# Last state product shared by three batches and added on VectorE, own products made ahead of the state

## The chip, the cores and the metric

The kernel runs on one core of one Trainium2 chip. All matrix products are in float32. The metric is the device time of one execution in microseconds (us); of several runs the median is taken. The engines are named as in the profile: PE is TensorE's matmul, PEld its weight load, DVE is VectorE, ACT is ScalarE, POOL is GpSimd, SP is SyncE, which issues the DMAs.

## The reference

Two layers act on x of 8 batches, 512 positions and 128 features. Each has an attention part and a feed-forward part with a layer norm, a modulation by a condition and a gated residual. Layer 0 has an RWKV mixing and a linear map with quantised operands, layer 1 a three-branch attention with 16 heads. The change touches only the last part, layer 1's feed-forward, a recurrence over the batches (B, with T = 512 rows each):

```python
def step(c, xt):
    ft = sigmoid(xt @ wf.T + c @ uf.T + bf)
    it = sigmoid(xt @ wi.T + c @ ui.T + bi)
    gt = tanh(xt @ wc.T + c @ uc.T + bc)
    return ft * c + it * gt, None
c_final, _ = lax.scan(step, c0, x)                 # x: the eight batches, one after the other
h = tanh(einsum('tbi,oi->tbo', x, wo) + c_final @ uo.T + bo)
...
h = layernorm(x) * (1 + cb) + sb                   # what the recurrence gets
x = x + gb * _L1_ffn_ref(h, ...)                   # the residual, and the output
```

Every batch's output needs the final state. So for each batch two products meet in a sum: its own, h times wo, and the product of the state with uo, which is the same for all batches.

## The kernel before

Features lie on the 128 partitions and the 512 positions of a batch on the free axis, so a batch is one 128x512 tile and a product of it fills one bank of PSUM. A float32 product of this size stands in the trace as two matmul records.

The main part is a loop over 192 units (batch, head group, kind of attention, rows of queries) in an order written out by hand. Three generators are advanced in its gaps: `layer0` (mixing and linear map of layer 0), `before` (norm and projections of layer 1, `prepare`, which stores a small latent tile through SP, L478) and `recurrence` (`recur`, L553). `recur` normalises a batch after its attention, makes h2 from it (L576), stores it to DRAM in `h2_all` (L578, all batches but the last), forms the three gate products (`of_state` L567 and L584), the gates (L586) and the state `cs2` (L591 to L595). `project` adds the attention's residual, and all batches but the last store their x in `x1_all` (L869).

The code around the change follows this loop (L1027 to L1056). Here a scheduler orders each engine's instructions. SP works through its DMAs strictly in order; a DMA that waits holds those behind it.

- `begin(b)` loads h2 of a batch (L1034) and its x (L1039), and makes the own product into a bank left open for a second product (L1042). The h2 tiles use the buffers qN and k0N of the attention's inputs. The five banks are `o` and `s0` to `s3`; the last batch takes h2 from `recur`.
- After the state, the loop of L1047 runs over the batches: state product into the same bank (L1051), tanh on ACT (L1053) into a tile `oT` (tag qR, two buffers), the gate gb on POOL (L1054), four transposes into one of three banks (L131) and the residual add on DVE (L133) in `add_residual`, and the store of the output (L1056).

PE's order before is: own product of batch 0, transposes of batch 7's attention residual, own product of batch 1, transposes of batch 7's norm (L126), the three gate products (L584), own products of 2, 3 and 4, and then state products, own products of 5, 6 and 7, and transposes mixed.

For the last batch the gate products take banks s0 to s2 and are read there by the tanhs of L586.

Of the kernel before, what the change touches and what calls it, by code (L numbers as in the profile page):

```python
# [11 lines left out]
FP = mybir.dt.float32  # L12
U32 = mybir.dt.uint32
AF = mybir.ActivationFunctionType
ALU = mybir.AluOpType
# [3 lines left out]
B, T, D = 8, 512, 128  # L19
NC = T // 128  # L20
# [3 lines left out]
HG = 4  # L24
# [25 lines left out]
def _views(t, cols):  # L50
    out, at = {}, 0
    for name, n in cols:
        out[name] = t[:, at : at + n]
        at += n
    return out
# [3 lines left out]
def adaln_kernel(ctx: ExitStack, tc: tile.TileContext, x, pa, pb, pc, pt, out):  # L59
    nc = tc.nc  # L60
    V, S, G, PE = nc.vector, nc.scalar, nc.gpsimd, nc.tensor
# [5 lines left out]
    WB, WC, WT = _views(wb, B_COLS), _views(wc, C_COLS), _views(wt, T_COLS)  # L67
# [9 lines left out]
    h2_all = [dram.tile([128, T], FP, name=f"h2all{b}") for b in range(B)]  # L77
    x1_all = [dram.tile([128, NC, D], FP, name=f"x1all{b}") for b in range(B)]
    small = ctx.enter_context(tc.tile_pool(name="small", bufs=2))
    pool_x = ctx.enter_context(tc.tile_pool(name="xs", bufs=5))  # L80
    xs = {}
# [46 lines left out]
    def add_residual(oT, ps, b):  # L128

        for c in range(NC):  # L130
            PE.transpose(ps[:, c * 128 : (c + 1) * 128], oT[:, c * 128 : (c + 1) * 128], ident)  # L131
        xb = xs[b].rearrange("p c d -> p (c d)")
        V.tensor_tensor(xb, ps, xb, ALU.add)  # L133
# [45 lines left out]
    pq = enter(tc.tile_pool(name="l1q", bufs=2))  # L179
    pi = enter(tc.tile_pool(name="l1i", bufs=1))  # L180
    pu = enter(tc.tile_pool(name="l1u", bufs=4))
    ps_s = enter(tc.tile_pool(name="ps_s", bufs=1, space=PSUM))
    ps_t = enter(tc.tile_pool(name="ps_t", bufs=3, space=PSUM))
    ps_o = enter(tc.tile_pool(name="ps_o", bufs=1, space=PSUM))

    def work(i, shape, name):


        return pw.tile(shape, FP, name=name, tag=i)

    def bank(shape, name):
        return ps_t.tile(shape, FP, name=name, tag="t")
# [355 lines left out]
    cs2 = state.tile([128, T], FP, name="cs2")  # L548
# [323 lines left out]
    made_of, latent_of, k1_of, chosen_of, q_of, k3_of, v_of, sel_of, out_of, acc_of, pT_of, rot_of, xnf_of, h2_of = ({} for _ in range(14))  # L872
# [54 lines left out]
    def need(name, b):  # L927
        while (name, b) not in ready:
            advance(M)
# [38 lines left out]
    for i in range(-2, len(units) + 3):  # L968
        un = units[i] if 0 <= i < len(units) else None
        ahead = units[i + 2] if i + 2 < len(units) else None  # L970
# [14 lines left out]
        if un:  # L985
            b, g = un.b, un.g
# [37 lines left out]
    ordered.close()  # L1024


    halves = {}  # L1027
    first = pi.tile([128, HG, T], FP, name="x1_first", tag="p3")

    def begin(b):  # L1030

        if b + 1 < B:
            h2_of[b] = pq.tile([128, T], FP, name=f"h2o_{b}", tag=("qN", "k0N")[b % 2])
            nc.sync.dma_start(out=h2_of[b], in_=h2_all[b])  # L1034
            if b < HG:
                xs[b] = first[:, b, :].rearrange("p (c d) -> p c d", d=D)
            else:
                xs[b] = pool_x.tile([128, NC, D], FP, name=f"x1_{b}", tag="x")
            nc.sync.dma_start(out=xs[b], in_=x1_all[b])  # L1039
        pool, tag = ((ps_o, "o"), (ps_s, "s3"), (ps_s, "s0"), (ps_s, "s1"), (ps_s, "s2"))[b % 5]  # L1040
        halves[b] = pool.tile([128, T], FP, name=f"ho_{b}", tag=tag)
        PE.matmul(halves[b], lhsT=WC["woT"], rhs=h2_of[b], start=True, stop=False)  # L1042

    for b in range(2):
        begin(b)
    need("recur", B - 1)
    for b in range(B):  # L1047
        for ahead in (b + 2, b + 3) if b == 0 else (b + 3,):
            if ahead < B:
                begin(ahead)  # L1050
        PE.matmul(halves[b], lhsT=WC["uoT"], rhs=cs2, start=False, stop=True)  # L1051
        oT = pq.tile([128, 2, T], FP, name=f"oT2_{b}", tag="qR")[:, 0, :]
        S.activation(oT, halves[b], AF.Tanh, bias=WC["bo"])  # L1053
        G.tensor_scalar(oT, oT, mod1[:, 5, b : b + 1], 1.0, ALU.mult, ALU.mult)  # L1054
        add_residual(oT, bank([128, T], f"rp2_{b}"), b)
        nc.sync.dma_start(out=out[b].rearrange("(c p) d -> p c d", p=128), in_=xs[b])  # L1056


def _packs(i):
# [70 lines left out]
```

## Time and profile before

| what | value |
|---|---|
| runs | median 1708.04 us of 3 (1707.66 to 1712.55) |
| profiled execution | 1708.48 us, its span 1706.7 us |
| PE, PEld, DVE, ACT, POOL busy | 92%, 55%, 74%, 68%, 55% of the span |
| granted TensorE clock, mean | 0.96 |
| last gate products begin | 1679.16 us |
| state ready (end of L595) | 1686.14 us |
| first state product | 1686.38 us |
| last residual add | 1702.79 to 1703.48 us |

Times inside an execution count from the start of the span. In lines of the timeline the first number is the start, the second the length, then engine, line, operation and tiles; in brackets is the engine's idle time before it, and what ended that. Lines of the chain have start, length, engine, tile, line and count: the chain is followed back from the last instruction, at each step to what released it. Stretches ("windows") list how long an engine was busy in them and the clock that the throttle granted to TensorE, 1.00 being full speed.

### The profile page before, as it was taken

The numbers are of one execution on the slowest core, as the hardware profiler recorded it, in microseconds if no ns is written. First come the engines' busy times: TensorE is split into PE (matmuls) and PEld (weight loads), VectorE is DVE, ScalarE is ACT, GpSimd is POOL, SyncE is SP. The second block draws the span as 40 slices with busy tenths as digits, with TensorE's granted clock in tenths as the row PEclk, the third lists the DMA queues.
The fourth block names the chain that finished last, engine by engine and source line by source line (L and its number), as shares of the span: only waits on it lengthen the run. The fifth ranks groups of instructions, "written<-read, shape, count | busy, mean of one in ns | idle before, by whom it ended". The sixth has DMA issues, their size and how long they took to land.

```text
span 1706.7 us, 39939 instructions
## 1 busy us (share of the span) xinstructions
PE 1572.7 (92%) x14777; PEld 938.1 (55%) x14777; DVE 1266.0 (74%) x4259; ACT 1152.8 (68%) x3245; POOL 936.8 (55%) x1370
## 2 busy tenths in 40 slices
PE   3388999899999999999899999989999999999997
PEld 2144655465555655655555555655555565665663
DVE  6678878875888868975979768867889667666543
ACT  2244787666776777777666677767776777777882
POOL 2155567554666547554656457654666456655551
PEclk8687999998999999999999999999999999999998
DMA  4000000000000000000000000000000000000012
GB/s 170 1 2 2 2 2 3 7 2 14 3 2 8 7 8 3 1 8 14 3 1 2 7 8 3 2 7 14 3 2 1 14 8 3 1 14 8 14 39 68
DMA packets 13778, 20.55 MB, mean 12 GB/s; under 512 B 912, under 2 KB 9104, under 8 KB 13456
## 3 DMA queue, kind: packets, MB, share of 16 engines
q1 hardware_dynamic: 13584, 17.99, 3.1%
q8 instruction: 118, 1.93, 0.5%
q14 instruction: 76, 0.62, 0.1%
HBM read 11.70 MB, written 5.77 MB: 10 GB/s over the span
## 4 chain that ended last, share of the span: by engine, by line
PE 63%; DVE 26%; ACT 5%; issue 3%; POOL 3%; DMA 0%; POOLq 0%; DVEq 0%; ACTq 0%
PE s L793 19%; PE t L837 12%; DVE p L805 7%; PE o L851 7%; PE s L755 2%; PE k3Rm L638 2%; PE qRm L638 2%; ACT p L814 2%; PE k3Np L610 1%; PE v1p L651 1%; PE op L862 1%; PE o L738 1%; PE qNp L610 1%; ACT pT L603 1%; POOL p L823 1%
## 5 line engine op out<-in xcount | busy, mean ns | idle before, releaser
L823 POOL TENSOR_SCALAR p<-p,rs 128x512 f32<-128x512 f32 (+3 forms) x1024 | 578.8, 586 | 390.9 <-DVE rs L819 221.9
L805 DVE CUSTOM_DVE_ANT_0 p<-s,mask 128x512 f32<-128x512 f32 (+3 forms) x1024 | 442.6, 477 | 178.4 <-PE s L793 178.0
L814 ACT ACTIVATE p<-p,nm 128x512 f32<-128x512 f32 (+3 forms) x1024 | 560.0, 553 | 11.9 <-DVE nm L805 11.8
L603 ACT COPY pT<-t 128x384 f32<-128x384 f32 (+1 forms) x768 | 354.8, 521 | 188.0 <-PE t L837 185.4
L837 PE MATMUL t<-ident,p 128*128 128x128 f32 x2560 | 367.4, 281 | 34.8 <-ACT pT L603 7.2
L837 PEld LDWEIGHTS t<-ident,p 128*128 128x128 f32 x2560 | 276.2, 142 | 160.3 <-issue 115.0
L814 ACT ACTIVATION_READ_ACCUMULATOR p<-p,nm 128x1 f32 x1024 | 197.2, 193 | 0.0
L793 PE MATMUL s<-k3R,qR 32*128 32x128 f32 (+3 forms) x2048 | 188.1, 458 | 4.4 <-DVE nm L805 3.2
L793 PE MATMUL s<-k1R,qR 32*128 32x512 f32 (+3 forms) x2048 | 185.9, 452 | 2.6 <-POOL k1R L625 2.5
L851 PE MATMUL o<-pT,v 128*32 128x512 f32 (+3 forms) x2048 | 153.2, 440 | 0.0
L793 PEld LDWEIGHTS s<-k3R,qR 32*128 32x128 f32 x2048 | 98.8, 188 | 84.4 <-DVE nm L805 30.9
L793 PEld LDWEIGHTS s<-k1R,qR 32*128 32x128 f32 x2048 | 105.4, 186 | 48.5 <-issue 13.6
L851 PEld LDWEIGHTS o<-pT,v 128*32 128x32 f32 x2048 | 60.4, 110 | 111.1 <-issue 100.3
L793 PE MATMUL s<-k0N,qN 32*128 32x512 f32 (+3 forms) x1024 | 102.3, 434 | 0.0
L793 PE MATMUL s<-k3N,qN 32*128 32x512 f32 (+3 forms) x1024 | 96.8, 434 | 0.0
L625 POOL TENSOR_TENSOR k3R<-k3R,rt_k3R 128x512 f32<-128x512 f32 x32 | 40.7, 1272 | 83.9 <-DVE rt_k3R L624 83.9
L805 DVE DVE_READ_ACCUMULATOR2_ANT nm<- 128x1 f32 x1024 | 82.8, 81 | 0.1
L765 POOL TENSOR_TENSOR p<-p,m 128x512 f32<-128x512 f32 x32 | 33.6, 1049 | 67.4 <-DVE m L764 67.4
L638 PE MATMUL qRm<-nqT,wb 96*128 96x512 f32 x128 | 68.8, 621 | 1.2 <-ACT nqT L475 0.7
L793 PEld LDWEIGHTS s<-k0N,qN 32*128 32x128 f32 x1024 | 60.5, 188 | 17.0 <-issue 2.5
L793 PEld LDWEIGHTS s<-k3N,qN 32*128 32x128 f32 x1024 | 55.1, 189 | 22.1 <-issue 15.2
L603 ACT COPY accT<-o 128x512 f32<-128x512 f32 x32 | 18.8, 587 | 71.0 <-PE o L851 71.0
(308 smaller groups left out, 2446.3 us busy)
## 6 DMA issues: line engine op xcount, KB each, us to landing
wb<-pb_dram SPq DMA_DIRECT2D x1, 3731.0 KB, 14.3
x<-x_dram SPq DMA_DIRECT2D x8, 256.0 KB, 3.7
x1all<-x SPq DMA_DIRECT2D x7, 256.0 KB, 2.0
h2all<-h SPq DMA_DIRECT2D x7, 256.0 KB, 2.0
h2o<-h2all SPq DMA_DIRECT2D x7, 256.0 KB, 2.6
x_first<-x1all SPq DMA_DIRECT2D x4, 256.0 KB, 3.6
out_dram<-x_first SPq DMA_DIRECT2D x4, 256.0 KB, 2.2
out_dram<-x SPq DMA_DIRECT2D x4, 256.0 KB, 2.3
```

What stands on the lines that cost most here:

```text
L603: S.copy(dst, src)
L610: PE.matmul(ps, lhsT=w[:, g * 128 : (g + 1) * 128], rhs=src, start=True, stop=True)
L625: G.tensor_tensor(lo, lo, r[0], ALU.subtract)
L638: PE.matmul(ps, lhsT=w[:, i * 128 : (i + 1) * 128], rhs=src, start=True, stop=True)
L755: PE.matmul(sp[h][to, :], lhsT=k[js, g, :], rhs=q[js, h * half : (h + 1) * half], start=(i == 0), stop=(i == 2), skip_group_check=True,)
L765: G.tensor_tensor(p2, p2, m2.unsqueeze(2).to_broadcast([128, T // 32, KEEP]), ALU.subtract)
L793: PE.matmul(un.s[j][:, at : at + n], lhsT=q[js, n - 128 : n], rhs=k[js, 0:n], start=(i == 0 and at == 0), stop=(i == 2), skip_group_check= ...
L805: V.tensor_tensor_reduce(out=un.p[:, j, at : at + n], in0=un.s[j][:, at : at + n], in1=mask[:, T - n :], scale=-1.0, scalar=3.4e38, op0=AL ...
L814: S.activation(p, p, AF.Exp, bias=un.nm[:, j, i : i + 1], scale=-1.0, accum_out=un.rs[:, j, i : i + 1])
L823: G.tensor_scalar(p, p, un.rs[:, j, i : i + 1], 1.0, ALU.mult, ALU.mult)
L837: PE.transpose(tp[:, k, :], un.p[:, j, at : at + 128], ident)
L851: PE.matmul(out_ps[js, c * 128 :], lhsT=v[:, c, js], rhs=pT[:, j, at[0] : at[-1] + 1 : step, :], start=not a and c == 0, stop=False, skip_ ...
```

## The change

- All seven h2 tiles get buffers of their own, those that layer 0's work used (tags l0 to l6), and all loads stand ahead of the products in the program.
- Batches 0, 2, 4, 6 and 7 keep their bank and the two products in it. Batches 1, 3 and 5 have their own product made into one of the three transposes' banks and copied by ACT to SBUF.
- The product of the state with uo is made once more into a bank `uo`; DVE adds it to the SBUF tiles of batches 1, 3 and 5, and tanh reads those.
- Own products of 0, 2, 1, 3 and 5 stand before the last norm on PE, those of 4, 6 and 7 between the gate products and the state.
- The transposes and the residual of a batch follow the tanh of the next in the program.

On PE the order becomes: own product of 0, transposes of the attention residual, own products of 2, 1, 3 and 5, transposes of the norm, gate products, own products of 4, 6 and 7; state product of 0, `uo`, state product of 2, transposes of 0, state product of 4, transposes of 1 and 2, state product of 6, transposes of 3, state product of 7, transposes of 4 to 7. On DVE the three adds of `uo` stand ahead of all eight residual adds. On SP the first five h2 loads stand behind the seventh batch's latent store, the sixth behind the sixth batch's h2 store and ahead of the eighth batch's latent store, the seventh behind the seventh batch's h2 store. Before, they stood behind that one, among the loads of x.

```diff
-    halves = {}
     first = pi.tile([128, HG, T], FP, name="x1_first", tag="p3")
+    for b in range(B - 1):
+        h2_of[b] = work(f"l{b}", [128, T], f"h2o_{b}")
+        nc.sync.dma_start(out=h2_of[b], in_=h2_all[b])
+    for b in range(B - 1):
+        if b < HG:
+            xs[b] = first[:, b, :].rearrange("p (c d) -> p c d", d=D)
+        else:
+            xs[b] = pool_x.tile([128, NC, D], FP, name=f"x1_{b}", tag="x")
+        nc.sync.dma_start(out=xs[b], in_=x1_all[b])
+
+    banks = {0: (ps_o, "o"), 2: (ps_s, "s3"), 4: (ps_s, "s0"), 6: (ps_s, "s1"), B - 1: (ps_s, "s2")}
+    sums = {}
 
     def begin(b):
-        if b + 1 < B:
-            h2_of[b] = pq.tile([128, T], FP, name=f"h2o_{b}", tag=("qN", "k0N")[b % 2])
-            nc.sync.dma_start(out=h2_of[b], in_=h2_all[b])
...
-        pool, tag = ((ps_o, "o"), (ps_s, "s3"), (ps_s, "s0"), (ps_s, "s1"), (ps_s, "s2"))[b % 5]
-        halves[b] = pool.tile([128, T], FP, name=f"ho_{b}", tag=tag)
-        PE.matmul(halves[b], lhsT=WC["woT"], rhs=h2_of[b], start=True, stop=False)
-
-    for b in range(2):
-        begin(b)
+        if b in banks:
+            pool, tag = banks[b]
+            sums[b] = pool.tile([128, T], FP, name=f"ho_{b}", tag=tag)
+            PE.matmul(sums[b], lhsT=WC["woT"], rhs=h2_of[b], start=True, stop=False)
+        else:
+            ps = bank([128, T], f"ho_{b}")
+            PE.matmul(ps, lhsT=WC["woT"], rhs=h2_of[b], start=True, stop=True)
+            sums[b] = work(f"p{b // 2}", [128, T], f"hs_{b}")
+            S.copy(sums[b], ps)
+
+    for b in (0, 2, 1, 3, 5):
+        begin(b)
     need("recur", B - 1)
-    for b in range(B):
-        for ahead in (b + 2, b + 3) if b == 0 else (b + 3,):
-            if ahead < B:
-                begin(ahead)
-        PE.matmul(halves[b], lhsT=WC["uoT"], rhs=cs2, start=False, stop=True)
-        oT = pq.tile([128, 2, T], FP, name=f"oT2_{b}", tag="qR")[:, 0, :]
-        S.activation(oT, halves[b], AF.Tanh, bias=WC["bo"])
+    for b in (4, 6, 7):
+        begin(b)
+    uo = bank([128, T], "uo")
+    oTs = {}
+
+    def finish(b):
+        if b in banks:
+            PE.matmul(sums[b], lhsT=WC["uoT"], rhs=cs2, start=False, stop=True)
+        else:
+            V.tensor_tensor(sums[b], uo, sums[b], ALU.add)
+        oT = oTs[b] = pq.tile([128, 2, T], FP, name=f"oT2_{b}", tag="qR")[:, 0, :]
+        S.activation(oT, sums[b], AF.Tanh, bias=WC["bo"])
         G.tensor_scalar(oT, oT, mod1[:, 5, b : b + 1], 1.0, ALU.mult, ALU.mult)
-        add_residual(oT, bank([128, T], f"rp2_{b}"), b)
-        nc.sync.dma_start(out=out[b].rearrange("(c p) d -> p c d", p=128), in_=xs[b])
+
+    for b in range(B + 1):
+        if b < B:
+            finish(b)
+        if b == 0:
+            PE.matmul(uo, lhsT=WC["uoT"], rhs=cs2, start=True, stop=True)
+        if b:
+            add_residual(oTs[b - 1], bank([128, T], f"rp2_{b - 1}"), b - 1)
+            nc.sync.dma_start(out=out[b - 1].rearrange("(c p) d -> p c d", p=128), in_=xs[b - 1])
```

More of the change, by code (lines that the diff above doesn't have):

```diff
@@ L1024, in adaln_kernel @@
     ordered.close()
-    halves = {}
     first = pi.tile([128, HG, T], FP, name="x1_first", tag="p3")
-    def begin(b):
-        if b + 1 < B:
-            h2_of[b] = pq.tile([128, T], FP, name=f"h2o_{b}", tag=("qN", "k0N")[b % 2])
-            nc.sync.dma_start(out=h2_of[b], in_=h2_all[b])
[L1035 to L1039, printed above, removed]
-        pool, tag = ((ps_o, "o"), (ps_s, "s3"), (ps_s, "s0"), (ps_s, "s1"), (ps_s, "s2"))[b % 5]
-        halves[b] = pool.tile([128, T], FP, name=f"ho_{b}", tag=tag)
-        PE.matmul(halves[b], lhsT=WC["woT"], rhs=h2_of[b], start=True, stop=False)
```

## The prediction

> **What bounds the kernel now.** I read the page first: PE is busy in 92% of the span, so PE work counts nearly everywhere. The diff, however, touches only what follows the last attention, so I then read the chain of work that ended last in the final 40 us, the timeline there, and the granted clock in stretches. The chain, whose columns are start, length and work:
>
> ```profile
> 1671.35 0.59 PE rp L131 x4
> 1671.96 0.70 DVE x L133
> ...
> 1676.65 0.36 DVE xnf L118
> 1677.01 0.04 issue
> 1677.05 1.26 PE tp L126 x4
> ...
> 1679.16 2.07 PE wfT L584 x2
> 1681.23 1.71 PE wiT L584 x2
> 1682.94 1.03 PE wcT L584 x2
> 1683.97 2.58 PE ho L1042 x6
> 1686.54 1.73 PE ho L1051 x4
> ...
> 1702.79 0.69 DVE x L133
> ```
>
> First comes a serial stretch (residual, norm, transposes, three gate products, state). Then, from 1686.4 on, PE has eight state products (L1051), three own products (L1042) and eight groups of transposes (L131). The timeline shows a batch's way through tanh, POOL and the transposes, and that ACT also waits for a transpose group:
>
> ```profile
> 1687.44 0.69 ACT L1053 ACTIVATE oT<-ho,wc 128x512 f32<-128x512 f32 x1 [2.75 <-PE ho L1051]
> 1688.22 0.69 POOL L1054 TENSOR_SCALAR oT<-oT,mod 128x512 f32<-128x512 f32 x1 [25.95 <-ACT oT L1053]
> ...
> 1698.58 0.69 ACT L1053 ACTIVATE oT<-ho,wc 128x512 f32<-128x512 f32 x1 [0.74 <-PE rp L131]
> ...
> 1699.36 0.69 POOL L1054 TENSOR_SCALAR oT<-oT,mod 128x512 f32<-128x512 f32 x1 [0.73 <-ACT oT L1053]
> ```
>
> oT has two buffers, so the tanh of batch b waits for the transposes of b-2. Last the clock, in stretches of 3.41 us (columns: window, length, PE busy, granted clock, DMA share, GB/s):
>
> ```profile
> 82.31:85.72 3.41, 1.54 (x6) 1.00 0.02 5
> 85.72:89.13 3.41, 3.41 (x5) 0.50 0.08 19
> 966.36:969.77 3.41, 1.70 (x26) 1.00 0.00 0
> 969.77:973.18 3.41, 3.05 (x8) 0.50 0.02 5
> 816.17:819.58 3.41, 1.89 (x20) 1.00 0.00 0
> 819.59:823.00 3.41, 2.75 (x56) 1.00 0.00 0
> 1672.92:1676.33 3.41, 0.00 (x0) 1.00 0.41 126
> 1676.34:1679.74 3.40, 1.82 (x5) 0.50 0.00 0
> 1679.74:1683.15 3.41, 3.41 (x5) 0.50 0.00 0
> 1683.16:1686.56 3.40, 3.40 (x9) 1.00 0.17 42
> ```
>
> The clock changes only at the ends of such stretches. A share of PE up to 0.50 (1.70 of 3.41) was followed by half clock, 0.55 (1.89) was not. Back to full it went after a full stretch. The gate products of the last batch run at half clock, because PE pauses from 1672.79 to 1677.05.
>
> **The change part by part.** Unit prices, all from this execution: a 128x512 product holds PE 0.865 (records at 1691.18 and 1692.04); product start to its tanh 1.06 (1686.38 to 1687.44); tanh 0.69, 0.09 to POOL, POOL 0.69, 0.06 to the transposes; these hold PE 0.49 (1698.68 to 1699.17), release DVE's add 0.70 after their start (1702.09 to 1702.79) and the oT buffer 0.76 after it (1697.82 to 1698.58).
>
> *Loads of h2 (seven, L1034 before).* They leave the buffers qN and k0N for those of layer 0's work, so SP issues five right after the seventh batch's latent store (1229.30). They wait for layer 0's last readers of those buffers; the transposes of oTf in the eighth batch end at 1342.53. At 0.32 each they are out by about 1344.2, and the next entry, the sixth batch's x1 store, goes at 1347.24 today. The sixth load stands behind the h2 store of 1370.70, waits about 2.0 for its landing, and has the latent store of 1409.24 behind it; the seventh follows the store of 1540.94. Cost 0: covers of 3 and 36 us. The loads that ran at 1671 and 1685 are gone, and nobody waited for them. The x1 loads keep their places between the same stores.
>
> *Own products of batches 2, 1, 3, 5 ahead of the norm.* PE had batch 1's here, ending at 1672.79; four from 1671.94 end at 1675.40, 1.65 before the transposes of 1677.05. Cost 0; without that cover each would cost 0.865. The three copies to SBUF on ACT (accT's copy of the same shape: 0.587) fall into ACT's idle 7.11 before h at 1678.33: cost 0, or 1.8 uncovered.
>
> *Own products of 4, 6, 7 between gates and state.* Three stand there today too. The last needs the bank of wcT, read by 1684.70; it would start at 1685.7. Cost 0, gain 0.
>
> *After the state.* Take the first state product (1686.38) as 0. Gone are three state products and three own products, added is one (uo): PE has 6 products instead of 11, 4.3 less. But the other engines have a chain of their own. Tanh 0 starts at 1.06, transposes 0 at 2.60 (behind uo and the product of batch 2). uo's sum is out at 1.93; the add for batch 1, 0.69 as the residual add of the same shape, lets tanh 1 start at 2.67, transposes 1 at 4.20. From here every batch waits for the buffer of the one two earlier: 0.76 + 0.69 + 0.09 + 0.69 + 0.06 = 2.29 from transposes to transposes. Batch 2: 4.89; 3: 6.49; 4: 7.18, but the product of batch 7 stands ahead on PE until 7.85; 5: 8.78; 6: 10.14; 7: 11.07. The last add starts at 11.77 and ends at 12.46. The adds for 3 and 5 end at 3.3 and 4.0, before their tanhs (4.96, 7.25); they delay the first residual add by about 0.7, for which nothing waits. Before the last tanh stands 0.34 without a visible cause (its product ended at 1700.20, it began at 1700.58); I keep it: 12.80. Today the same stretch takes 1703.48 - 1686.38 = 17.10. **Gain 4.30**; bounds 4.64 (no such gap) and 3.6 (below).
>
> *The stores of the output.* The last one's issue, landing and program end take 3.2 after the last add today. Stores now come every 1.1 us instead of 1.4 to 2.0; landings go from 2.2 to 3.0 today, so 0 to 0.7 more. I take 0, since the last add follows the one before by 1 us and a store of 256 KB at the 296 GB/s seen at 1701 needs 0.9.
>
> *The clock.* The stretch 1672.92 to 1676.33 now holds 2.48 of PE work and keeps full clock. Then the four transposes take 0.70 instead of 1.28 and the first gate product starts at 1678.58. The stretch to 1679.74 now holds about 0.66 + 1.16 = 1.82 of work, 0.53: between 0.50, which lost the clock, and 0.55, which kept it. If it is lost at 1679.74, the gates end at 1682.62, full clock is back at 1683.15, and three own products end at 1685.48: 0.9 earlier than today. If it is kept, the state is ready at 1683.6 and its first product starts at 1683.8: 2.6 earlier. The phase of these stretches against the program may differ between runs; shifting it through 3.41 us, the same arithmetic gives anything from 0.5 later to 2.6 earlier, with 0.9 near the middle. I take **0.9**, ends -0.5 and 2.6.
>
> **Sum.** 4.3 + 0.9 = 5.2. The profiled execution took 1708.48 (span 1706.7 and 1.8 around it), so it would become 1703.3. It lies 0.44 above the median of the runs, so for a median 1708.04 - 5.2 = **1702.8**. 0.3% of this time, 5.1 us or a border at 1702.9, is about what a measurement of this kernel can tell from no change: the three runs of before reach from 1707.66 to 1712.55.
>
> **Rivals.** *A, above:* shorter tail, clock lost for part of the gates: 1702.8, own range 1702.0 to 1703.5.
>
> *B, the clock stays up.* For it: the pauses left are 1.65 and 0.88. Against it: the share of 0.53, and most phases give a lower one. 4.3 + 2.6 = 6.9, 1701.1. The Trainium skill (TensorE: Matmul & The Clock Gate, Part 1) has the clock fall after an idle window of some 3.4 us; by that, neither pause would cost it and B would be the outcome. The trace agrees on the width, but 82.31 to 85.72 was 45% busy and the clock fell all the same.
>
> *C, no gain from the clock.* The stretch boundary falls so that it is lost at 1677 or 1678. Only the tail gains: 4.3 less 0.3, 1704.0; with slower landings 1704.7.
>
> *D, SP's queue holds the last latent.* This is the slower one. Six loads are queued ahead of the eighth batch's latent store (1409.24), and that batch's first use is its k0N product at 1489.44. Should a load wait for something later than the transposes of 1342.53, PE waits one for one beyond about 1487; the change comes out slower once the queue is held past 1492, and at 1500 it is 1708.04 - 5.2 + 13 = 1715.8. Against it: every reader of those buffers belongs to layer 0, which the eighth batch leaves before its latent exists.
>
> *E, the change does less than it says:* PE stays the bound in the tail, because products and transposes collide. 6 products and 8 groups are 5.2 + 3.9 = 9.1 of 12.5, so this would need 3 us of collisions; 1705 to 1706.
>
> **Chances.** A 0.38, B 0.28, C 0.24, E 0.05, D 0.05. The range takes A, B and C with their bounds: 1700.8 (4.64 + 2.6) to 1705.2 (C at its worst, with some spread of runs). Faster by over 0.3%: B, and somewhat over half of A, and a little of C: 0.54. Within 0.3%: the rest of A and C, and E: 0.40. Slower: D and a disturbed main part, 0.06.
>
> **What would show it.** In the profile after: five h2 loads near 1342 to 1344; PE work until 1675.4 and copies on ACT before h; granted clock 1.00 between 1676.3 and 1679.7 where it was 0.50; a first transposes group about 2.6 and a last add about 12.5 after the first state product; ACT waiting for rp L131, not for ho. Wrong would be: tanhs waiting for DVE, stores landing late, a stretch of half clock inside the tail, or any change before 1671.

## The result, and the profile after

| | before | changed |
|---|---|---|
| runs | median 1710.03 us (1707.34 to 1712.84, 6 runs) | median 1702.41 us (1700.13 to 1705.39, 6 runs) |
| ratio to before | | 0.9958, 95% interval 0.9947 to 0.9970 |
| profiled execution | 1708.48, span 1706.7 | 1705.39, span 1703.6 |

By the ratio the change saves 7.2 us (5.1 to 9.1). By a 2% bound the two are the same; by the 0.3% that this kernel's measurement can tell, the changed one is faster.

The two profiled executions differ by 3.1 only. The profiled one of the changed kernel is the slowest of its six runs, the one of before lies near the fast end of its own. So I cut both traces at events that exist in each: the first transpose of the last attention residual (rp L131), the first state product, and the end of the last residual add.

| us | before | changed | predicted |
|---|---|---|---|
| start to the first residual transpose | 1671.27 | 1673.21 | no change |
| first residual transpose to first state product | 15.11 | 14.69 | 14.21 |
| first state product to end of last add (the tail) | 17.10 | 12.47 | 12.80 |
| last add to the end of the span | 3.19 | 3.22 | 3.19 |
| the three parts behind the first transpose | 35.40 | 30.38 | 30.20 |

The region that the change touches became 5.02 shorter. The rest, 1.94 longer, lies ahead of it; it is taken up below. The chain of the changed kernel that ended last, in the same stretch as the one shown of before (start, length, engine, tile, line, count):

```profile
1673.29 0.59 PE rp L131 x4
1673.91 0.70 DVE x L133
...
1678.59 0.36 DVE xnf L118
1679.08 1.02 PE tp L126 x4
1680.12 0.79 ACT h L576
1680.95 1.25 PE wfT L584 x2
1682.21 1.71 PE wiT L584 x2
1683.91 1.58 PE wcT L584 x2
1685.49 2.58 PE ho L1045 x6
1688.07 0.86 PE ho L1062 x2
1688.93 0.87 PE uo L1073 x2
1689.82 0.70 DVE hs L1064
1690.55 0.73 ACT oT L1066
...
1699.68 0.69 DVE x L133
```

wiT at 1.71 and most of wcT (1.58) still run at half clock; the three own products (ho, 2.58) take 0.86 each. After the state, the chain leaves PE at once, by the sum of batch 1 on DVE (L1064) and its tanh. The timeline of ACT shows what the later tanhs wait for (in brackets the idle time before and its end):

```profile
1690.55 0.72 ACT L1066 ACTIVATE oT<-hs,wc 128x512 f32<-128x512 f32 x1 [0.90 <-DVE hs L1064]
...
1692.85 0.72 ACT L1066 ACTIVATE oT<-hs,wc 128x512 f32<-128x512 f32 x1 [0.92 <-PE rp L131]
1693.53 0.69 ACT L1066 ACTIVATE oT<-ho,wc 128x512 f32<-128x512 f32 x1
1695.15 0.72 ACT L1066 ACTIVATE oT<-hs,wc 128x512 f32<-128x512 f32 x1 [0.94 <-PE rp L131]
1696.46 0.69 ACT L1066 ACTIVATE oT<-ho,wc 128x512 f32<-128x512 f32 x1 [0.58 <-PE rp L131]
1697.46 0.69 ACT L1066 ACTIVATE oT<-ho,wc 128x512 f32<-128x512 f32 x1 [0.32 <-PE rp L131]
```

The four later waits are all for transposes, that is for one of the two oT buffers; only the first is for a DVE add. The stretches of the clock (window, length, PE busy, granted clock, DMA share, GB/s):

```profile
1674.99:1678.40 3.41, 2.32 (x6) 1.00 0.01 2
1678.41:1681.82 3.41, 1.87 (x6) 1.00 0.00 0
1681.83:1685.23 3.40, 3.40 (x5) 0.50 0.00 0
1685.24:1688.64 3.40, 3.40 (x9) 1.00 0.00 0
```

One stretch of half clock is left of two. It follows a stretch in which PE was busy for 1.87 of 3.41, a share of 0.55.

The loads of h2, in the timeline of SP's queue:

```profile
1303.96 40.93 SPq L1030 DMA_DIRECT2D h2o<-h2all  x5
1349.21 0.32 SPq L869 DMA_DIRECT2D x1all<-x  x1
...
1374.71 0.32 SPq L1030 DMA_DIRECT2D h2o<-h2all  x1
```

The last of the five is out at 1344.9. The x1 store follows 1.97 later than before (1347.24 then) and the eighth batch's latent store, at 1411.20, 1.96 later (1409.24 then), which is the 1.94 that this execution is late anyway.

**Where the 1.94 comes from.** accT is the attention's sum, which ACT copies out of PSUM 32 times in the main part. From the start to the first of these copies, in code that the change does not touch, the changed kernel took 179.23 and before 176.78, 2.45 more; from there to the last one 1491.44 and 1491.95. The stretches of the start-up show the clock, first before, then the changed kernel (columns as above, windows of 42):

```profile
42.00:84.00 42.00, 16.01 (x48) 0.60 0.00 0
84.00:126.00 42.00, 36.87 (x237) 0.89 0.01 3
126.00:168.00 42.00, 34.60 (x295) 0.79 0.01 1
```

```profile
42.00:84.00 42.00, 17.95 (x44) 0.54 0.00 0
84.00:126.00 42.00, 36.38 (x193) 0.80 0.01 3
126.00:168.00 42.00, 33.29 (x313) 0.88 0.01 1
```

Between 42 and 126 the clock was lower in the execution of the changed kernel; in the first 168 us it spent 81.9 at half clock, before 75.1. Over the eleven profiles of this study, all with the same start-up, the first accT copy comes between 176.1 and 182.4, and the time at half clock in the first 168 us lies between 71.7 and 95.6; the latest copy (182.4) goes with the most half clock (95.6), but among the others the order is loose (176.1 goes with 75.1 and 78.5, 176.9 with 71.7). So the clock is the likely cause of the late start, and no run tested it. Either way single executions are several us apart before the changed code is reached, and the sum of a change of 5 us has to be read from its own region, or from many runs.

### The profile page after: what moved, and what is told of

Its sections match the earlier page's. It is cut to its first block, busy times and chain, and to the rows that moved or that the text cites. A ratio compares the mean times of both kernels' runs of the same rounds, so it can differ in the third digit from the quotient of the medians.

```text
span 1703.6 us, 39936 instructions
## 1 busy us (share of the span) xinstructions
PE 1571.0 (92%) x14773; PEld 936.0 (55%) x14773; DVE 1267.4 (74%) x4262; ACT 1154.0 (68%) x3248; POOL 936.7 (55%) x1370
## 4 chain that ended last, share of the span: by engine, by line
PE 63%; DVE 26%; ACT 5%; issue 3%; POOL 3%; DMA 0%; POOLq 0%; SPq 0%; ACTq 0%; DVEq 0%
PE s L793 19%; PE t L837 12%; DVE p L805 7%; PE o L851 7%; PE s L755 2%; PE k3Rm L638 2%; PE qRm L638 2%; ACT p L814 2%; PE k3Np L610 1%; PE v1p L651 1%; PE op L862 1%; PE o L738 1%; PE qNp L610 1%; PE k0Np L610 1%; ACT pT L603 1%
```

## The experiments

The theory: the gain is the shorter tail, 4.6, whose new bound is the chain through the two oT buffers, plus part of the gates at full clock. Rivals are that PE's count of products sets the tail, that the loads or the stores take part, and that the pauses are too short to lose the clock. The kernels e1, e2 and e6 were timed once only, so for them the profile counts alone. All columns below are from the profiles of the runs, cut as in the table above.

| kernel | first transpose to state | tail | to the end | sum | half clock ahead of the state |
|---|---|---|---|---|---|
| before | 15.11 | 17.10 | 3.19 | 35.40 | 6.8 |
| changed | 14.69 | 12.47 | 3.22 | 30.38 | 3.4 |
| e8, changed again | 14.69 | 12.48 | 3.23 | 30.40 | 3.4 |
| e1, three products | 14.70 | 16.11 | 3.21 | 34.02 | 3.4, and again in the tail |
| e2, six buffers | 15.98 | 11.57 | 3.20 | 30.75 | 6.8 |
| e3, pause filled | 13.00 | 12.49 | 3.22 | 28.71 | none |
| e4, before, pause filled | 13.00 | 17.11 | 3.20 | 33.31 | none |
| e5, before, early loads | 15.11 | 17.10 | 3.19 | 35.40 | 6.8 |
| e6, six buffers, products ahead | 14.69 | 10.35 | 4.59 | 29.63 | 3.4 |
| e7, e6 and pause filled | 13.00 | 10.35 | 4.50 | 27.85 | none |
| e9, e7, first store earlier | 13.00 | 10.41 | 4.37 | 27.78 | none |

### Without the shared product

Batches 1, 3 and 5 each get a state product of their own in place of `uo`; everything else of the change stays.

```diff
-    uo = bank([128, T], "uo")
...
-            V.tensor_tensor(sums[b], uo, sums[b], ALU.add)
+            own = bank([128, T], f"uo_{b}")
+            PE.matmul(own, lhsT=WC["uoT"], rhs=cs2, start=True, stop=True)
+            V.tensor_tensor(sums[b], own, sums[b], ALU.add)
...
-        if b == 0:
-            PE.matmul(uo, lhsT=WC["uoT"], rhs=cs2, start=True, stop=True)
```

> Each of the batches 1, 3 and 5 gets a state product of its own, in a bank of the transposes, and its add on DVE; the rest stays as changed. PE has 8 state products after the state, not 6. The stretch counts from the start of the first state product to the end of the last residual add: 17.10 us before, 12.47 after. Theory (sharing pays because tanh, POOL, transposes and the two oT buffers form a chain, and every product put into it delays the chain by more than its own time): 15.5. Rival (only PE's own time counts): 12.47 + 2 x 0.865 = 14.2. Rival (sharing is worth nothing, the gain came from the own products moved away): 12.5.

Measured: tail 16.11, one time of 1705.81. Two more products are 1.73 of PE, but the tail grew by 3.64: the products for batches 3 and 5 stand behind transposes on PE, and the tanhs wait for their adds. ACT's timeline:

```profile
1691.27 0.72 ACT L1067 ACTIVATE oT<-hs,wc 128x512 f32<-128x512 f32 x1 [2.52 <-DVE hs L1065]
1691.89 0.67 ACT L1067 ACTIVATE oT<-ho,wc 128x512 f32<-128x512 f32 x1
1695.16 0.72 ACT L1067 ACTIVATE oT<-hs,wc 128x512 f32<-128x512 f32 x1 [2.60 <-DVE hs L1065]
```

Part of the excess is the clock: the stretch from 1695.66 to 1699.07 was busy for 1.38 of 3.41, and the last transposes ran at 0.50.

```profile
1699.00 1.09 PE L131 MATMUL rp<-ident,oT 128*128 128x128 f32 x4 [0.96 <-POOL oT L1068]
```

1.09 instead of 0.66, so 0.43 of the 16.11. Without it 15.7 stands near the 15.5 expected of the chain, and far from both rivals. Hence in this order of PE the sharing carries about 3.2 of the tail's gain of 4.63, and the rest of the change (the own products moved ahead of the state, the new order of the transposes) about 1.4; these two were not taken apart.

### Six oT buffers

```diff
-        oT = oTs[b] = pq.tile([128, 2, T], FP, name=f"oT2_{b}", tag="qR")[:, 0, :]
+        oT = pq.tile([128, 2, T] if b % 3 == 0 else [128, T], FP, name=f"oT2_{b}", tag=("qR", "qN", "k0N")[b % 3])
+        oT = oTs[b] = oT[:, 0, :] if b % 3 == 0 else oT
```

> oT gets six buffers instead of two, the order on PE as the scheduler gives it; the rest stays as changed. Theory (the two buffers set the pace after the change): the same stretch falls from 12.47 to 11.7, no tanh waits for a transposes group any more, and the last batch then waits for its state product, which stands late on PE. Rival (PE or DVE sets the pace already): 12.4 to 12.5.

Measured: tail 11.57, one time of 1704.20. No tanh waits for transposes any more; the last two wait for their state product, since PE's order puts it behind the transposes of earlier batches. ACT's timeline:

```profile
1692.68 0.72 ACT L1067 ACTIVATE oT<-hs,wc 128x512 f32<-128x512 f32 x1
1694.14 0.69 ACT L1067 ACTIVATE oT<-ho,wc 128x512 f32<-128x512 f32 x1 [0.75 <-PE ho L1062]
1696.31 0.69 ACT L1067 ACTIVATE oT<-ho,wc 128x512 f32<-128x512 f32 x1 [1.48 <-PE ho L1062]
```

So the two buffers were the bound of the changed tail, and the price of their chain is 0.90. The gates fared worse in this execution: the clock was lost for two stretches, and the state came 0.87 later than before's. The stretches, columns as in those of the changed kernel:

```profile
1675.21:1678.62 3.41, 1.56 (x6) 1.00 0.00 0
1678.62:1682.03 3.41, 2.62 (x3) 0.50 0.00 0
```

The edit does not touch the gates. What differs is where the stretches lie: here one ends 0.12 after the first residual transpose, in every other profile of the study 1.5 to 2.1 after it.

### The pause filled, with the change and without

Two products that nobody reads (512 and 384 columns) fill PE between the own products and the norm's transposes; in the kernel before, five of them. They are extra work; the outputs do not depend on them.

```diff
     for b in (0, 2, 1, 3, 5):
         begin(b)
+    idle = bank([128, T], "idle")
+    for n in (512, 384):
+        PE.matmul(idle[:, 0:n], lhsT=WC["woT"], rhs=h2_of[0][:, 0:n], start=True, stop=True)
     need("recur", B - 1)
```

> The changed kernel, with two products that nobody reads (512 and 384 columns, 1.5 us) between the own product of batch 5 and the transposes of the last norm, so that PE's pause of 1.65 us ahead of them closes. Theory (the clock is lost in a stretch of 3.41 us in which PE is busy for half or less): granted clock 1.00 through the gate products whatever the phase; from the start of the residual's transposes of the last attention to the first state product 12.5 us, where after has 14.69 and before 15.11; time 1 to 2 below the changed kernel. Rival (the clock is lost for another reason, or each pause of 0.9 is enough): 14.7 and the time of the changed kernel.

> The kernel before, with products that nobody reads (four of 512 columns and one of 256, 3.9 us) in PE's pause ahead of the transposes of the last norm, and nothing else. It takes the clock's part of the change alone. Theory: granted clock 1.00 through the gates, 12.5 us from the residual's transposes to the first state product instead of 15.11, the stretch from there to the last add stays 17.1, the time is 2.6 below before. Rival (clock plays no part): 15.1 and 17.1, the time of before.

Measured: e3 ratio 0.9952 (0.9936 to 0.9967), median 1701.44; e4 0.9991 (0.9979 to 1.0003), median 1707.37. In both profiles the gates run at full clock and the state comes 13.00 after the first transpose, 2.11 earlier than before; the expectation had 12.5. For e4, 2.1 lies within the timed interval of -0.5 to 3.6, which holds zero too: its runs alone do not show the gain, its profile does. The stretches of e3 over the pause and the gates, their ends counted back in steps of 3.413 from the next change of its clock at 1696.50:

```profile
1676.02:1679.43 3.41, 2.27 (x8) 1.00 0.00 0
1679.43:1682.84 3.41, 3.41 (x10) 1.00 0.00 0
```

The timeline of e3 shows what holds the state at 13.00:

```profile
1676.43 1.12 DVE L118 TENSOR_SCALAR xnf<-x,mv_r,lrs_r 128x128 f32<-128x128 f32 x4
1676.92 1.01 PE L126 MATMUL tp<-ident,xnf 128*128 128x128 f32 x4 [0.27 <-DVE xnf L118]
...
1678.80 1.12 PE L584 MATMUL wfT<-h,wc 128*128 128x512 f32 x2 [0.87 <-ACT h L576]
```

DVE makes the norm's output in four pieces in 1.12, and the transposes follow it piece by piece: 1.01 at full clock against 1.24 at half clock in before. The first gate product comes 7.75 after the first residual transpose (7.89 before), with the clock up as with the clock down.

### The loads alone

The kernel before, with the seven h2 loads ahead of its products, into the buffers of layer 0's work.

```diff
+    for b in range(B - 1):
+        h2_of[b] = work(f"l{b}", [128, T], f"h2o_{b}")
+        nc.sync.dma_start(out=h2_of[b], in_=h2_all[b])
     def begin(b):
         if b + 1 < B:
-            h2_of[b] = pq.tile([128, T], FP, name=f"h2o_{b}", tag=("qN", "k0N")[b % 2])
-            nc.sync.dma_start(out=h2_of[b], in_=h2_all[b])
```

> The kernel before, with only the loads of h2 moved as in the change: buffers l0 to l6 of layer 0's work, loads ahead of the products in the program. Theory (the loads had nobody waiting for them): first state product to last add 17.1 us as before, the main part unchanged, the time that of before within 1 us. Rival (the earlier loads make the main part or the tail faster, which would explain why the changed kernel's runs lie 6 to 7 us below before where its end shows 5): 1 to 2 us below before.

Measured: ratio 0.9995 (0.9983 to 1.0007); the three parts of the region are 15.11, 17.10 and 3.19 as in before, to the hundredth, and between the first and the last copy of accT lie 1491.58 (1491.95 before). No gain or cost of the loads shows.

### Products ahead, and both remedies together

Six oT buffers as above, and all state products issued early: PE's order becomes product 0, `uo`, products 2, 4 and 6, transposes of 0 and 1, product 7, the other transposes. e7 adds the filled pause.

```diff
-        if b in banks:
-            PE.matmul(sums[b], lhsT=WC["uoT"], rhs=cs2, start=False, stop=True)
-        else:
+        if b not in banks:
             V.tensor_tensor(sums[b], uo, sums[b], ALU.add)
...
+    ahead = {0: (0, -1, 2, 4), 1: (6,), 3: (7,)}
     for b in range(B + 1):
+        for n in ahead.get(b, ()):
+            PE.matmul(uo if n < 0 else sums[n], lhsT=WC["uoT"], rhs=cs2, start=n < 0, stop=True)
         if b < B:
             finish(b)
-        if b == 0:
-            PE.matmul(uo, lhsT=WC["uoT"], rhs=cs2, start=True, stop=True)
```

> The changed kernel with six buffers for oT, and the state products issued earlier in the program: those of 0, uo, 2 and 4 ahead of the first tanh, that of 6 with batch 1, that of 7 with batch 3. Theory (with the buffers gone the late product of batch 7 was next, and after it DVE, which has 3 + 8 adds of about 0.68): first state product to last add 11.0, against 12.47 changed and 11.57 with six buffers alone; the last four residual adds follow each other without a pause. Rival (PE sets the pace): 11.6.

> The kernel of the run with six buffers and earlier state products, and the filled pause (512 and 384 columns that nobody reads) added: both remedies at once. Theory (independent): 13.0 from the residual's transposes to the first state product, 11.0 from there to the last add, together 24.0 where before has 32.2 and after 27.2; 8.2 below before, 2 to 4 below the changed kernel, by the phase of the clock. Rival (one eats the other, or the stores of the output become the end): above 25.

Measured: the last add ends 10.35 after the first state product in both, less than the 11.0 expected, and the last four residual adds follow each other on DVE without a pause. For e7 that makes 23.35 to the last add, where 24.0 was expected. But the end then takes 4.59 and 4.50 instead of 3.2, so that e6, with 14.94 from state to end, is no better than e2 with 14.77: the stores become the end, as the rival for e7 had it, but behind the last add, where its sign of "above 25" does not look. The stretches of e7 (window, length, busy time of PE, PEld, DVE, ACT and POOL, granted clock, DMA share, GB/s):

```profile
1690.00:1691.00 1.00, 1.00 (x10) 0.79 (x9) 1.00 (x2) 0.21 (x1) 1.00 (x3) 1.00 1.15 346
...
1693.00:1694.00 1.00, 0.00 (x0) 0.00 (x0) 0.58 (x1) 0.00 (x0) 0.00 (x0) 1.00 1.12 335
...
1695.00:1696.00 1.00, 0.00 (x0) 0.00 (x0) 0.00 (x0) 0.00 (x0) 0.00 (x0) 0.88 0.96 290
```

From 1690 to 1696 the DMA engines are full at 285 to 346 GB/s, and they go on for three microseconds after the last add. The eight stores are 2.1 MB, and at about 300 GB/s that is an estimated 7 us, of the 9.1 from the first store to the end: the stores have become the bound. e7 nevertheless has the lowest ratio of the study, 0.9943 (0.9927 to 0.9960), median 1700.20 (1699.62 to 1702.68), though its interval overlaps those of e3 and of the changed kernel; by the sum of the region it is 2.5 below the latter. On the same chip the changed kernel gave:

> The changed kernel as it is, for the size of its gain and a further look at the clock's phase. Theory: 12.5 from the first state product to the last add in every execution, 13.0 to 16.0 ahead of it by the phase of the clock (14.7 in the first profile); 4.6 of the gain fixed and 0 to 2 from the clock, so 4.5 to 6.5 below the kernel before in the mean. Rival (a part of the gain lies elsewhere): 7 or more.

Measured: 0.9964 (0.9951 to 0.9977), median 1704.70 (1703.16 to 1706.14), with the first execution's tail and state to 0.01.

### The first store earlier

e7, with state products 4 and 6 behind the transposes of batch 0.

```diff
-    ahead = {0: (0, -1, 2, 4), 1: (6,), 3: (7,)}
+    ahead = {0: (0, -1, 2), 2: (4, 6), 3: (7,)}
```

> The kernel with six buffers and the filled pause, its state products placed so that the transposes of batch 0 come right after the first three (0, uo, 2), then products 4 and 6, transposes of 1, product 7, and the other transposes. In the two runs with the products ahead the last add came 10.35 us after the first state product, but 4.5 to 4.6 passed from there to the end of the span, where it was 3.2 otherwise, and the DMA engines were full from the first store on. Theory (there the eight stores set the end, and they began late, since the first transposes stood behind five products): first store about 0.8 us earlier, last add 10.4 to 11.0, 3.2 to 3.8 to the end, together 14.0 where that order has 14.9 and six buffers alone 14.8. Rival (the stores go at their own pace, or the last add decides): 14.8 again.

Measured: ratio 0.9958 (0.9942 to 0.9974), median 1702.61; 10.41 and 4.37, together 14.78 against e7's 14.85. That is the rival's 14.8, not the 14.0 of the theory. The first store goes out 4.4 after the first state product (5.7 in e7), but the time won is not kept: the second and third go out at 6.2 and 7.5, where e7 has 6.3 and 7.4. Stretches of e9, columns as for e7:

```profile
1691.00:1692.00 1.00, 1.00 (x7) 0.62 (x5) 0.52 (x1) 1.00 (x3) 1.00 (x2) 1.00 0.63 191
1692.00:1693.00 1.00, 1.00 (x9) 0.85 (x8) 0.39 (x2) 0.96 (x2) 1.00 (x3) 1.00 0.24 71
...
1695.00:1696.00 1.00, 0.44 (x4) 0.20 (x2) 1.00 (x3) 0.00 (x0) 0.00 (x0) 1.00 1.15 345
```

The DMA engines have work early, and then stand at a share of 0.24 until the following adds are done; the last stores queue up as in e7. An order that keeps them fed from 4.4 on was not tried, so how much less than 14.8 is possible stays open.

## Why the prediction was right, point by point

- **After the state, 4.30.** Measured 4.63, tail 12.47. The chain through the two buffers was worked out as 12.46 and holds at each batch: transposes 0 at 2.59 (2.60 predicted), 1 at 4.21 (4.20), 4 at 7.86 (7.85), 7 at 11.09 (11.07). Batches 2, 3, 5 and 6 lie within 0.06 of it too. The term was mis-sized by the 0.34 before the last tanh: I carried a gap without a visible cause from one kernel into another. It did not come back, and what made it in before stays open. Six buffers confirm the mechanism by 0.90, three products in place of one the worth of the sharing.
- **The clock, 0.9.** Measured 0.42. The case taken as the likeliest, A, came true: clock 1.00 through the norm's transposes (until 1681.82, in an execution that is 1.94 late), then lost for one stretch within the gates. The failed step is "the four transposes take 0.70 instead of 1.28". They took 1.01, bound by DVE's four norm pieces, and started 0.09 later after those: the first gate product stood at 7.74 after the first residual transpose where 7.31 was predicted. With 7.74 put into the prediction's arithmetic, and half clock from 8.61 to 12.02 as measured, the 5.17 of gates and own products end at 7.74 + 0.87 + 3.41 + (5.17 - 0.87 - 1.70) = 14.62; the trace has 14.69. The same 0.43 is missing from B: 2.11 measured with the clock up, 2.6 predicted.
- **The phase.** The prediction spread the phase of the stretches over all of 3.41 and called 0.9 "near the middle". The profiles do not spread: in ten of the eleven a stretch ends 1.5 to 2.1 after the first residual transpose, in e2 0.12 after it. Counted from the start of the span the ends are spread, from 0.07 to 2.75 (remainder by 3.41), so the program has taken its place against the stretches by then; how was not studied. So A, worked out with the phase of before's profile, was the usual case and not one of many: the changed kernel's two profiles, e1 and e6 all have 14.69 or 14.70. The averaging over phases gave no reason for that.
- **Rival B.** Five profiles of the changed code without the filling (the changed kernel twice, e1, e2, e6) lost the clock behind pauses of about 1.8 and 0.87; the stretches before the loss were busy for 1.87, 1.75, 1.82, 1.56 and 1.82 of 3.41. The four profiles with a filled pause (e3, e7 and e9 of the changed code, e4 of the code before) kept it, and their stretches over the pauses were busy for 2.26 or 2.27. So the pause ahead of the transposes is what loses the clock here, and the filling shows it. The prediction's limit between 0.50 and 0.55 of a stretch is not sharp, however. In the changed kernel's own trace the stretch from 818.25 to 821.66 was busy for 1.86 and kept the clock, the one from 1678.41 for 1.87 and lost it; e2 kept it after 1.66 (1173.45 to 1176.86), e4 lost it after 1.96 (1280.48 to 1283.89), and before's trace, from which the limit was read, lost it once after 3.00 (119.85 to 123.26). That a share of 0.53 was a toss-up was right; the busy time alone does not settle it. The Trainium skill (TensorE: Matmul & The Clock Gate, Part 1) names an idle window of about 3.4 us as what drops the clock; the traces agree on the length of the window, not on its having to be idle.
- **Rival C** is what e2 shows: 1.56 of 3.41, clock lost at the beginning of the gates and for two stretches. "No gain from the clock" was too good by 0.87 there, and so was the lower end of -0.5 given for the term; 0.43 of that is the transposes again.
- **Loads, 0, and rival D.** Right; e5 shows it alone. Only the last of the five went near the time worked out (1344.58, in an execution that is 1.94 late); the first left at 1303.96 already, since each waited for a reader of its own and not all for the last.
- **Own products, 0.** Right: their copies end on ACT 2.20 before h, and PE pauses 1.77 before the norm's transposes (1.65 predicted). That the moved products also feed the clock is the 0.42 above.
- **Stores, 0.** Right at 3.22. The worry behind the bound of 0.7 came true two steps further, in e6 and e7.
- **Rival E** falls with the tail of 12.47 and ACT's waits.
- **Sum 5.2, measured 5.02 in the region.** Part of this closeness is luck: the tail was 0.33 better than predicted, the clock's part 0.48 worse, and the two nearly cancel. The predicted 1702.8 is closer to the median of 1702.41 than its parts deserve for another reason too: the three runs that it started from had a median of 1708.04, and larger sets of before gave 1708.41 to 1710.03. The timed gains are 7.2 (5.1 to 9.1) and 6.2 (3.9 to 8.4, e8); 5.02 lies just below the first interval and inside the second. The profiles show no gain in the main part that would make up the rest: from the first to the last copy of accT ten of the eleven took 1491.3 to 1492.0, with the change and without (e2 1493.0). The start-up, which varies by 6, is the same code in all, so the rest is probably its chance; the runs don't show that.

## What to carry to other kernels

When PE's work at the end of a kernel is cut, follow one tile through all engines and count its buffers: here the new bound was a chain through two buffers, worked out to within 0.06 at every batch, then PE's order, and then the stores' bandwidth. A short serial stretch ahead of a burst of products can cost twice if PE rests in it: here 1.5 us of unread products in the pause were worth 1.7 us. Terms can be wrong in opposite directions and still add up, so compare each one with its own stretch of the trace. A change of 5 us in a kernel whose start-up varies by 6 is judged by cutting the traces at common events.

## What the runs showed of the hardware

- The granted clock changed only at the ends of stretches of 3.41 us. Ahead of the gates it fell after stretches with PE busy for 1.56 to 1.87 of it, with no pause longer than about 1.8 us, and it fell even inside a tail of transposes (1.38, e1).
- Over all eleven traces, every stretch at full clock that was busy for less than 1.66 by the records was followed by half clock (126 of them). Between 1.66 and 1.96 both happened (33 kept it, 15 lost it). Above that only four were followed by half clock (2.57 in e1 and e2, 2.82 in e2, 3.00 in before).
- A stretch at half clock that was busy for 2.62 (e2) was followed by another at half clock. Fully busy ones did not always end it either: in before three of them follow each other from 389.50 to 399.73, all at 0.50, before the clock came back.
- Eight stores of 256 KB close together moved at 285 to 346 GB/s, and stretched the end from 3.2 to 4.5.
